# Dilated attention, then a binary 3x3 depthwise convolution: block 0's convolution without TensorE, and the residual laid into PSUM

## The chip, the cores and the metric

The kernel runs on one core of one Trainium2 chip. Its time is the device time in microseconds, the median of several runs; lower is better. The engines are named TensorE (PE in the profile), VectorE (DVE), ScalarE (ACT), GpSimd (POOL) and SyncE (SP, which issues most of the DMAs).

## What is computed

The input is x, 16 images of 56 x 56 pixels with 384 channels, all float32. Two residual layers follow each other:

```python
x = x + conv0(_gn(x), w_qkv, w_proj, b_proj)   # layer 0
x = x + conv1(_gn(x), w)                       # layer 1
# _gn: per image, 32 groups of 12 channels, mean and variance over pixels and channels of the group
# conv0: qkv = einsum('bchw,oc->bohw'); 3 dilations (1, 2, 3) of 128 channels, 4 heads of 32 each;
#        for each pixel softmax over its 9 dilated neighbours of q.k / sqrt(32), then the weighted sum of v;
#        then einsum('bhwc,oc->bhwo', y, w_proj) + b_proj
# conv1: depthwise 3x3, zero padding, the weights replaced by their signs
```

## The kernel before

**Tiling.** Channels lie on the 128 partitions, so an image has three channel blocks (0, 1, 2). Pixels lie along the free axis. A chunk is 8 rows of one image, 448 pixels; an image has 7 chunks, the whole input 112. Each chunk m goes through three plans.

- `plan_a` (lines 494 to 547) loads the chunk, turns it to channels on partitions (`pt_x`, L515), copies it out (L528), takes the statistics of layer 0's normalisation (L530) and stores it as `xd`.
- `plan_b` (549 to 762) is layer 0. It loads and normalises xn (L563), projects k, v (`pkv`) and the queries (`pq`, both L567), copies k and v out (L580) and exchanges their border rows with the neighbouring chunks by DMA (L588, L589). For each of 9 combinations of dilation and neighbour row VectorE multiplies q and k for three neighbours at once (`t`, L632), and TensorE sums over the head's channels (`ps`, L613). The softmax goes through a copy (`sT`, L652), a transpose (`pt_s`, L656) and VectorE and ScalarE steps; the weights, split into three bfloat16 terms (L675 to L683), are transposed by a DMA (`aT`, L686). For each of 9 combinations TensorE spreads the weights over the head's channels (`pb_a`, L700), VectorE multiplies them by v (`w`, L711), and GpSimd adds up (L721, L724, L725 to `y`). `out_project` (731 to 750) multiplies y by the projection weights (`po`, L738); VectorE adds the bias and the residual `xr` (L743) and takes the statistics of layer 1's normalisation (L747); SyncE stores the chunk as `x1d` (L750).
- `plan_c` (775 to 1000) is layer 1, and starts ten chunk steps later, once the image's statistics are there. Block 2's taps are made by ScalarE from a normalised, padded copy (`zg`, L912; `m`, L934) and summed by GpSimd (L944, L949, L952). Blocks 0 and 1 work on `x1`, which isn't normalised: the scale and offset of the normalisation go into per-channel scalars `cs` (`column_scalars`, L764), and ScalarE lays the middle tap, the residual and the offset into a PSUM tile `pc` (`column`, L852). TensorE adds columns of taps to it (`convolve`, L862): it multiplies a packed copy `z`, which holds three shifted rows of 32 channels on 96 partitions (loaded by three DMAs per block, L814, and normalised by ScalarE, L829), by diagonal matrices `kdiag`. Of block 1 it makes the left and the right column of taps (8 products, four at a time on separate quarters of the array), of block 0 the right column only (`LEFT = (0,)`, 4 products). VectorE adds the rest in place (L880) and writes the last tap's result back to x1 (L883): 5 instructions for block 0, 2 for block 1. Then TensorE turns the chunk back (`pt_o`, L961), ScalarE copies it (`osb`, L967), SyncE stores it (L970).

**The last image** (index 15) has its own forms: block 2's nine taps are on VectorE (`taps_last`, L925), and z lies in buffers of other pools (`z_last`).

**PSUM.** Pool `ps_mt` has two banks, which pkv, pt_x, pt_s, po, pt_o and the statistics' products share in turn; `ps_q` has two for pq and pc; `ps_s` has one for ps and the exponentials; `ps_bc` holds one pb_a of three banks. Two products at the start (`open_banks`, L1018) write ps_q's banks over 448 columns.

**Order.** Each piece of work of a chunk has a time in the table `WHEN` (lines 35 to 66), in units of which `STEP` = 9 make a chunk. Chunk m's piece is emitted at its time plus 9 m (plan_c: plus 90 more). The pieces are sorted by time, and between times 81 and 1022 each engine's instructions are pinned in this order (`pin`, L1046), SyncE's queue too. Outside it the framework's scheduler orders by priority. A piece of several stages is a generator: each `yield` ends a stage, and each stage has its own time. The engines run in order and wait on semaphores.

Of the kernel before, what the change touches and what calls it, by code (L numbers as in the profile page):

```python
# [8 lines left out]
F32 = mybir.dt.float32  # L9
# [8 lines left out]
P = 128  # L18
HEADS = 4
HD = 32  # L20
# [3 lines left out]
LEFT = (0,)  # L24
# [11 lines left out]
    load_in=[[21.699]],  # L36
    turn_in=[[22.335, 22.469, 24.701, 28.875], [23.943, 25.409, 27.06, 27.63], [28.352, 28.363, 28.599,
        33.075]],
    load_x=[[-7.77]],
    normalise=[[-1.597], [-3.05], [-3.143]],  # L40
    k=[[1.392, 1.555, 1.762], [3.751, 3.762, 5.408], [3.97, 4.507, 7.411]],
    v=[[11.109, 11.185, 12.149], [14.632, 15.913, 18.706], [17.166, 18.74, 20.057]],
    query=[[10.432], [14.052], [17.994]],
    score=[[11.334], [12.68], [13.826], [14.44], [15.484], [16.643], [18.961], [18.981], [19.283]],
    burst=[[15.151], [18.93], [19.682]],
    softmax=[[20.163, 20.314, 20.448, 20.459, 20.882, 20.893, 21.29, 21.784, 22.998, 23.194]],
    weigh=[[24.063, 24.321, 27.605], [27.904, 27.915, 28.335], [28.245, 28.256, 28.346], [28.64, 28.697,
        28.708], [28.701, 29.148, 29.922], [29.172, 29.776, 32.964], [30.222, 30.929, 35.033], [31.47, 31.924,
        35.101], [33.982, 34.952, 36.663]],
    load_residual=[[37.899]],  # L50
    out_project=[[38.334, 38.803, 38.814, 140.965], [39.193, 39.204, 39.638, 45.624], [39.633, 39.644, 40.418,
        44.585]],
    load_g=[[23.473]],
    normalise_g=[[28.853]],
    taps=[[29.551, 30.093], [30.192, 30.638], [31.25, 32.971]],
    sums=[[36.467], [36.6], [36.611]],
    load_x1=[[21.201]],
    load_z=[[16.673, 19.532], [15.429, 23.495]],
    normalise_z=[[21.293, 22.164], [23.971, 24.249]],
    column=[[21.708], [24.774]],  # L60
    convolve=[[22.545, 23.258], [24.904, 25.733]],
    turn_out=[[36.858, 36.869, 36.88], [37.053, 37.1, 37.526], [37.486, 37.56, 37.792], [37.575, 37.599,
        39.723]],
    statistics=[[47.11, 48.584, 52.665, 52.676, 53.263, 53.274, 54.624, 54.703, 54.714, 54.82, 55.967, 56.105,
        56.694, 57.245, 57.256]],
# [6 lines left out]
def dilated_attention_then_binary_conv(  # L72
# [78 lines left out]
    PARTS = JG * NQ  # L151
# [34 lines left out]
    kcol = const.tile([P, JG, 6], F32, name="kcol")  # L186

    kdiag = const.tile([K3, 2, JG * NQ, HD], F32, name="kdiag")
# [19 lines left out]
    packed = to_pack[:, : JG * P].rearrange("p (j g) -> p j g", j=JG)  # L208
    fold = to_pack[:, JG * P : (JG + 1) * P].rearrange("p (a c) -> p a c", c=HD)
    nc.gpsimd.memset(to_pack, 0.0)  # L210
    for part in range(PARTS):
        j, q = divmod(part, NQ)
        g0, c0 = part * HD // GN_CH, GN_G + 4 * part
        for g in range(NG):
            nc.gpsimd.tensor_copy(gsel[:, g, c0 : c0 + 4], gsel[:, g, g0 : g0 + 4])
        nc.gpsimd.tensor_copy(packed[q * HD : (q + 1) * HD, j, c0 : c0 + 4], gsel[q * HD : (q + 1) * HD, j, g0 : g0 + 4])
# [6 lines left out]
    for j in range(JG):  # L223
        nc.tensor.matmul(
            pz[:, :P], packed[:, j], fold.rearrange("p a c -> p (a c)"), start=(j == 0), stop=(j == JG - 1)
        )
# [79 lines left out]
    def small_weights():  # L306
# [31 lines left out]
        up, mid, down = (ktap[:, :JG, o] for o in (1, 4, 7))  # L338
        nc.vector.tensor_add(kcol[:, :, 0], mid, down)
        nc.vector.tensor_add(kcol[:, :, 1], kcol[:, :, 0], up)  # L340
        nc.vector.tensor_add(kcol[:, :, 2], up, mid)
        by_row = ktap[:, :JG].rearrange("p j (y x) -> p j y x", x=3)[:, :, :, 0]
        for of, ys in ((0, (1, 2)), (1, (0, 1, 2)), (2, (0, 1))):
            for n, y in enumerate(ys):
                nc.vector.tensor_add(kcol[:, :, 3 + of], by_row[:, :, y], kcol[:, :, 3 + of if n else of])
# [7 lines left out]
        for kx in (0, 2):  # L353
            nc.vector.tensor_tensor(
                kdiag[:, kx // 2],
                kp[:, kx, : JG * NQ].unsqueeze(2).to_broadcast([K3, JG * NQ, HD]),
                eye3.unsqueeze(1).to_broadcast([K3, JG * NQ, HD]),
                ALU.mult,
            )
# [20 lines left out]
    def group_norm(sets):  # L380
# [70 lines left out]
        mrz = both[:K3, n_mr:].rearrange("p (j q s) -> p j q s", j=JG, q=NQ) if n_z else None  # L451
# [15 lines left out]
    def put(t0, what, piece):  # L467

        places = WHEN[what]
        for n, stages in enumerate(places):  # L470
            of_it = (n,) if len(places) > 1 else ()
            if len(stages) == 1:
                at(t0 + stages[0], lambda of_it=of_it: piece(*of_it))
                continue
            steps = piece(*of_it)
            for when in stages:
                at(t0 + when, lambda steps=steps: next(steps, None))
# [71 lines left out]
    def plan_b(m, t0):  # L549
# [181 lines left out]
        def out_project(j):  # L731
# [4 lines left out]
            po = ps_mt.tile([P, 512], F32, tag="mt", name="po")  # L736
            for g in range(NG):
                nc.tensor.matmul(  # L738
                    po[:, :PX], wprojT[:, g, j * P : (j + 1) * P], had[f"y{g}"], start=(g == 0), stop=(g == NG - 1)
                )  # L740
            yield
            xr = had["xr"]
            nc.vector.scalar_tensor_tensor(  # L743
                xr[:, j, :], po[:, :PX], bias[:, j : j + 1], xr[:, j, :], op0=ALU.add, op1=ALU.add
            )
# [18 lines left out]
    def column_scalars(b):  # L764

        mr = mr1[b][0]
        cs = st_p.tile([P, JG, 12], F32, tag="cs", name="cs")
        scale, offset = mr[:, :JG, 1:2], mr[:, :JG, 0:1]
        nc.gpsimd.tensor_tensor(cs[:, :, 0:3], ktap[:, :JG, 1:NTAP:3], scale.to_broadcast([P, JG, 3]), ALU.mult)
        nc.gpsimd.tensor_tensor(cs[:, :, 6:9], ktap[:, :JG, 0:NTAP:3], scale.to_broadcast([P, JG, 3]), ALU.mult)  # L770
        nc.gpsimd.tensor_tensor(cs[:, :, 3:6], kcol[:, :, 0:3], offset.to_broadcast([P, JG, 3]), ALU.mult)
        nc.gpsimd.tensor_tensor(cs[:, :, 9:12], kcol[:, :, 3:6], offset.to_broadcast([P, JG, 3]), ALU.mult)
        nc.gpsimd.tensor_scalar(cs[:, :, 1], cs[:, :, 1], 1.0, None, op0=ALU.add)
        cs1[b] = cs

    def plan_c(m, t0):
# [5 lines left out]
        def zero(j):  # L782
            for z, _, _ in had[f"z{j}"]:
# [10 lines left out]
        def set_of(j, q):  # L794
            return next(z[:, q - q0] for z, q0, q1 in had[f"z{j}"] if q0 <= q < q1)

        def load(j):
            by_set = x1d[b].rearrange("(j q c) n -> j c q n", q=NQ, c=HD)[j]
            if b < B - 1:
                z = z_p.tile([P, NQ * PX], F32, tag="z", name="z")[:K3].rearrange("p (q n) -> p q n", q=NQ)  # L800
                had[f"z{j}"] = [(z, 0, NQ)]
            else:

                had[f"z{j}"] = []
                for q0 in range(0, NQ, 2):
                    pool, tag = (t_p, "t") if c % 2 == 0 else (w_p, "w") if (j, q0) != (1, 2) else (xr_p, "xr")
                    z = pool.tile([P, 3, PX], F32, tag=tag, name="z_last")[:K3, :2]
                    had[f"z{j}"].append((z, q0, q0 + 2))
            for ky in range(3):
# [3 lines left out]
                for z, q0, q1 in had[f"z{j}"]:  # L813
# [4 lines left out]
            zero(j)  # L818

        def normalise(j):  # L820
            mrz = mr1[b][1]
            for q in range(NQ):
                z = set_of(j, q)
                if q == NQ - 1 and b == B - 1:
                    nc.vector.tensor_scalar(
                        z, z, mrz[:, j, q, 1:2], mrz[:, j, q, 0:1], op0=ALU.mult, op1=ALU.add
                    )
                    continue
                nc.scalar.activation(z, z, AF.Identity, bias=mrz[:, j, q, 0:1], scale=mrz[:, j, q, 1:2])  # L829
            yield  # L830
            zero(j)
# [10 lines left out]
        def column(j):  # L842
# [4 lines left out]
            parts = [(0, 1, 3), (1, ROWS, 4)] if c == 0 else [(0, ROWS, 4)]  # L847
            if c == NCH - 1:
                parts = [(0, ROWS - 1, 4), (ROWS - 1, ROWS, 5)]
            for r0, r1, of in parts:  # L850
                for x0, x_end, more in ((1, W, 6), (0, 1, 0)) if j in LEFT else ((0, W, 0),):
                    nc.scalar.activation(  # L852
                        pcr[:, r0:r1, x0:x_end], x1[:, j, r0 + 1 : r1 + 1, x0:x_end], AF.Identity,
                        bias=cs[:, j, of + more : of + more + 1], scale=cs[:, j, 1:2],
                    )

        def convolve(j):
            pcr = rows(had["pc", j][:, :PX])

            def tap(kx, q):  # L860
                x0, x1 = max(0, 1 - kx), W - max(0, kx - 1)
                return nc.tensor.matmul(  # L862
                    pcr[q * HD : (q + 1) * HD, :, x0:x1], kdiag[:, kx // 2, j * NQ + q, :],
                    rows(set_of(j, q))[:, :, x0 + kx - 1 : x1 + kx - 1], start=False, stop=(kx == 2),
                    skip_group_check=True,
                )

            in_one_go([
                lambda kx=kx, q=q: tap(kx, q) for kx in ((2,) if j in LEFT else (0, 2)) for q in (3, 0, 1, 2)
            ])  # L870
            yield
            x1 = had["x1"][:, j]
            mid = x1[:, 1 : ROWS + 1]
            cs, above, below = cs1[b], 1 if c == 0 else 0, ROWS - 1 if c == NCH - 1 else ROWS
            taps = [(above, ROWS, 0, 0, 0)]
            if j in LEFT:
                taps += [(above, ROWS, 0, 6, 1), (0, ROWS, 1, 7, 1), (0, below, 2, 8, 1)]
            for r0, r1, ky, at_, left in taps:
# [221 lines left out]
```

## Time and profile before

| | |
|---|---|
| median of 3 runs | 5014.38 us (5013.85 to 5015.21) |
| the profiled execution | 5018.26 us, its span from first to last instruction 5015.4 us |
| granted TensorE clock, mean over the span | 0.977 |
| TensorE busy | 4840.0 us, 97% of the span |
| VectorE busy | 4483.8 us, 89% |
| GpSimd busy | 4239.8 us, 85% |
| ScalarE busy | 2571.0 us, 51% |
| DMA, mean | 167 GB/s |

The profile gives busy time by engine, by stretch of the span and by group of instructions. A group's row has the line, the engine, the operation, written tile <- read tiles with their shapes, the number of instructions, then their busy time, the mean of one in ns, and the idle time of the engine just before them with what ended it. A float32 matmul has two records, a bfloat16 one has one. TensorE's weight loads (PEld) are listed apart and lie beside the products. Because matmuls are pipelined and their ends are modelled, the start of the next burst says more about the price of a burst than its length.

### The profile page before, as it was taken

What the parts mean: (1) busy time and instruction counts of PE and PEld (TensorE: products, weight loads), DVE (VectorE), ACT (ScalarE), POOL (GpSimd) and SP (SyncE); (2) the same over time, 40 slices, a digit from 0 to 9 for tenths busy, and PEclk for the clock granted to TensorE, in tenths of its full rate; (3) what the DMA queues carried; (4) which work ended last, traced back from release to release, by engine and by line L of the source; (5) the groups of instructions that cost most, each with busy time, mean ns of one, the idle gap of its engine ahead of it and who ended that gap; (6) DMA issues with size and microseconds to landing.
All of it is one profiled execution on the core that took longest, in us unless ns stands there. A gap on an engine that the chain in (4) does not pass through costs nothing.

```text
span 5015.4 us, 69405 instructions
## 1 busy us (share of the span) xinstructions
PE 4840.0 (97%) x23469; PEld 2230.2 (44%) x23469; DVE 4483.8 (89%) x4711; ACT 2571.0 (51%) x4645; POOL 4239.8 (85%) x2951
## 2 busy tenths in 40 slices
PE   7999999999999999999999999999999999999954
PEld 4444444444444444444444444444444444444421
DVE  4888999999999999999999999999999999999846
ACT  3222555555555555555555555555555555555455
POOL 2677889888898989988888898989989898998970
PEclk9999999999999999999999999999999999999965
DMA  5434666666666666666666666666666666655554
GB/s 173 119 106 125 177 173 175 175 174 177 179 178 177 173 175 171 178 177 177 174 173 175 176 178 179 180 175 171 175 179 175 177 175 177 161 145 146 133 144 142
DMA packets 813945, 836.23 MB, mean 167 GB/s; under 512 B 362643, under 2 KB 782870, under 8 KB 813590
## 3 DMA queue, kind: packets, MB, share of 16 engines
q1 hardware_dynamic: 805606, 819.81, 61.1%
q10 hardware_dynamic: 7984, 12.00, 0.7%
q8 instruction: 185, 3.03, 0.3%
q14 instruction: 170, 1.39, 0.1%
HBM read 477.43 MB, written 231.21 MB: 141 GB/s over the span
## 4 chain that ended last, share of the span: by engine, by line
PE 83%; POOL 7%; issue 2%; DVE 2%; ACT 1%; DMA 0%; SPq 0%; ACTq 0%; POOLq 0%; DVEq 0%
PE pkv L567 27%; PE po L738 14%; PE pq L567 13%; PE ps L613 11%; PE pb_a L700 5%; PE pc L862 5%; PE pt_o L961 3%; POOL w L721 3%; PE pt_x L515 2%; PE pt_s L656 1%; POOL m L944 1%; DVE w L711 1%; DVE t L632 1%; POOL y L724 1%; POOL y L725 1%
## 5 line engine op out<-in xcount | busy, mean ns | idle before, releaser
L721 POOL TENSOR_TENSOR w<-w 128x1344 f32<-128x1344 f32 x672 | 2053.2, 3055 | 148.2 <-DVE w L711 103.3
L711 DVE TENSOR_TENSOR w<-pb_a,v 128x1344 f32<-128x1344 f32 x1008 | 1562.4, 1550 | 200.0 <-PE pb_a L700 125.4
L567 PE MATMUL pkv<-xn,wqkvT 128*128 128x448 f32 x3924 | 1593.2, 546 | 0.0
L632 DVE TENSOR_TENSOR t<-pq,k 128x1344 f32<-128x1344 f32 x1008 | 1546.4, 1545 | 11.8 <-PE ps L613 7.3
L567 PEld LDWEIGHTS pkv<-xn,wqkvT 128*128 128x128 f32 x3924 | 718.7, 190 | 646.9 <-issue 643.7
L944 POOL TENSOR_TENSOR m<-m 128x1344 f32<-128x1344 f32 x210 | 642.6, 3060 | 273.2 <-ACT m L934 273.0
L738 PE MATMUL po<-y,wprojT 128*128 128x448 f32 x2016 | 823.3, 553 | 12.4 <-ACT osb L967 7.6
L567 PE MATMUL pq<-xn,wqkvT 128*128 128x448 f32 x1962 | 808.2, 547 | 0.1
L580 ACT COPY v<-pkv 128x448 f32<-128x448 f32 x336 | 180.0, 536 | 985.2 <-PE pt_o L961 493.4
L613 PE MATMUL ps<-t,sel 128*32 128x448 f32 x6048 | 662.0, 547 | 3.6 <-DVE t L632 2.9
L829 ACT ACTIVATE z<-z,mr 96x448 f32<-96x448 f32 x840 | 569.7, 750 | 7.3 <-DMA z<-x1d 7.3
L934 ACT ACTIVATE m<-zg,ktap 128x448 f32<-128x448 f32 x945 | 549.7, 657 | 5.4 <-POOL m L944 4.7
L567 PEld LDWEIGHTS pq<-xn,wqkvT 128*128 128x128 f32 x1962 | 360.2, 190 | 395.3 <-issue 285.7
L738 PEld LDWEIGHTS po<-y,wprojT 128*128 128x128 f32 x2016 | 359.5, 191 | 347.3 <-issue 256.5
L967 ACT COPY osb<-pt_o 112x384 f32<-112x384 f32 x420 | 191.4, 481 | 433.7 <-PE pt_o L961 420.4
L724 POOL TENSOR_TENSOR y<-w 128x448 f32<-128x448 f32 x336 | 382.4, 1138 | 29.7 <-PE po L738 4.2
L700 PE MATMUL pb_a<-aT,spread 24*128 24x448 bf16 x3024 | 369.5, 360 | 37.2 <-DVE w L711 27.7
L725 POOL TENSOR_TENSOR y<-y,w 128x448 f32<-128x448 f32 x336 | 381.9, 1137 | 26.0
L880 DVE SCALAR_TENSOR_TENSOR pc<-x,cs,pc 128x440 f32<-128x440 f32 (+3 forms) x560 | 375.8, 673 | 26.8 <-issue 8.6
L700 PEld LDWEIGHTS <-spread 24*128 24x128 bf16 x3024 | 99.6, 91 | 462.0 <-issue 396.8
L613 PEld LDWEIGHTS ps<-t,sel 128*32 128x32 f32 x6048 | 169.6, 109 | 297.8 <-issue 286.2
L580 ACT COPY k<-pkv 128x448 f32<-128x448 f32 x336 | 179.4, 534 | 222.6 <-PE pkv L567 220.3
(154 smaller groups left out, 4671.1 us busy)
## 6 DMA issues: line engine op xcount, KB each, us to landing
z<-x1d SPq DMA_DIRECT2D x570, 224.0 KB, 4.4
xr<-xd SPq DMA_DIRECT2D x112, 672.0 KB, 5.8
x1d<-xr SPq DMA_DIRECT2D x112, 672.0 KB, 5.2
xn<-xd SPq DMA_DIRECT2D x109, 672.0 KB, 5.4
xin<-in_x_dram SPq DMA_DIRECT2D x105, 672.0 KB, 6.2
xd<-xa SPq DMA_DIRECT2D x315, 224.0 KB, 3.4
out_dram<-osb SPq DMA_DIRECT2D x420, 168.0 KB, 3.4
x<-x1d SPq DMA_DIRECT2D x80, 560.0 KB, 4.6
```

Of the source, the lines that this page charges most:

```text
L567: nc.tensor.matmul(dst[:, :PX], wqkvT[:, cc, o0 : o0 + P], had["xn"][:, cc, :], start=(cc == 0), stop=(cc == NG - 1))
L613: return nc.tensor.matmul(had["ps"][32 * j : 32 * j + 32, :PX], sel[:, s0 : s0 + 32], tk, start=(issued[j] == 1), stop=(issued[j] == len(r ...
L632: nc.vector.tensor_tensor(t.rearrange("p k (r w) -> p k r w", w=W), q3, k3, ALU.mult)
L700: return nc.tensor.matmul(pb[:, kx, :PX].rearrange("p (s n) -> p s n", s=NSUB), spread[rows_of, v % 2, :], had["a"][rows_of, :, v // 8, :] ...
L711: nc.vector.tensor_tensor(w.rearrange("p k (r w) -> p k r w", w=W), pb[:, :, :PX].rearrange("p k (r w) -> p k r w", w=W), three(kv[1][g][m ...
L721: nc.gpsimd.tensor_tensor(w0, w0, w, ALU.add)
L724: nc.gpsimd.tensor_tensor(y, w0[:, 0], w0[:, 1], ALU.add)
L725: nc.gpsimd.tensor_tensor(y, y, w0[:, 2], ALU.add)
L738: nc.tensor.matmul(po[:, :PX], wprojT[:, g, j * P : (j + 1) * P], had[f"y{g}"], start=(g == 0), stop=(g == NG - 1))
L829: nc.scalar.activation(z, z, AF.Identity, bias=mrz[:, j, q, 0:1], scale=mrz[:, j, q, 1:2])
L934: nc.scalar.activation(rows(t[:, kx]), zp[:, ky : ky + ROWS, kx : kx + W], AF.Copy, scale=ktap[:, JG, o : o + 1])
L944: nc.gpsimd.tensor_tensor(had["m"], had["m"], t, ALU.add)
```

## The change

- Block 0 (`CB = 1` is the only block with products now) has no z, no load of it, no normalisation of it and no products. ScalarE's `column` lays the interior columns and the two border columns with bias scalars of their own (three pieces instead of two), and VectorE adds seven taps in place and writes the eighth back, each tap a stage of its own. `kcol`, `cs`, `kdiag` and the small packing tensors of the statistics change size accordingly.
- `out_project` takes `po` from `ps_q` instead of `ps_mt`. ScalarE first lays residual plus bias into it; the three products add to that (`start=False`); ScalarE copies the sum to `xr`. VectorE's addition is gone; its statistics stay.
- `WHEN` is another table: block 0's convolution has eight stages, the projection five; k's projection of a chunk is emitted at -8.9 to -6.4 instead of 1.4 to 7.4, the store of a chunk of x1 at 30.6 instead of 44.6, the output's stages at 39.6 to 43.4 instead of 36.9 to 39.7. The statistics of the first two images have times of their own.

Core of the diff, with the taps of block 0:

```diff
-LEFT = (0,)
+CB = 1
...
-            po = ps_mt.tile([P, 512], F32, tag="mt", name="po")
+            po = ps_q.tile([P, 512], F32, tag="q", name="po")[:, :PX]
+            xr = had["xr"]
+            nc.scalar.activation(po, xr[:, j, :], AF.Identity, bias=bias[:, j : j + 1])
+            yield
...
-            yield
-            xr = had["xr"]
-            nc.vector.scalar_tensor_tensor(
-                xr[:, j, :], po[:, :PX], bias[:, j : j + 1], xr[:, j, :], op0=ALU.add, op1=ALU.add
-            )
+            yield
+            nc.scalar.copy(xr[:, j, :], po)
             yield
             nc.vector.bn_stats(stats1[b][:, j, c, :], xr[:, j, :])
...
-                for x0, x_end, more in ((1, W, 6), (0, 1, 0)) if j in LEFT else ((0, W, 0),):
+                for x0, x_end, more in ((1, W - 1, 0), (0, 1, 3), (W - 1, W, 6)) if j < CB else ((0, W, 0),):
...
-            in_one_go([
-                lambda kx=kx, q=q: tap(kx, q) for kx in ((2,) if j in LEFT else (0, 2)) for q in (3, 0, 1, 2)
-            ])
-            yield
...
+            if j >= CB:
+                in_one_go([lambda kx=kx, q=q: product(kx, q) for kx in (0, 2) for q in (3, 0, 1, 2)])
+                yield
+                tap(0, 1)
+                yield
+            else:
+                for ky, kx in ((0, 1), (0, 0), (1, 0), (2, 0), (0, 2), (1, 2), (2, 2)):
+                    tap(ky, kx)
+                    yield
+            tap(2, 1, mid)
...
-    query=[[10.432], [14.052], [17.994]],
+    query=[[1.5], [2.982], [3.688]],
...
-    out_project=[[38.334, 38.803, 38.814, 140.965], [39.193, 39.204, 39.638, 45.624], [39.633, 39.644, 40.418,
-        44.585]],
+    out_project=[[23.391, 25.515, 26.174, 27.604, 79.334], [25.765, 26.049, 26.586, 27.934, 68.996], [26.354,
+        27.424, 27.849, 29.998, 30.603]],
...
-    convolve=[[22.545, 23.258], [24.904, 25.733]],
+    convolve=[[27.149, 29.154, 29.175, 29.74, 29.751, 29.762, 29.773, 29.836], [32.213, 32.574, 32.949]],
```

In it `tap(ky, kx, to)` is one VectorE `scalar_tensor_tensor`: a shifted window of x1 times one column of `cs`, plus the PSUM tile, written back to the PSUM tile or to `to`.

## The prediction

> **What bounds the kernel now.** I read the busy time by stretch first, the groups by shape second, then TensorE's and VectorE's timelines over one chunk. Busy time in five stretches, columns as in the heading:
>
> ```profile
> core 0: us, PE busy (x) PEld busy (x) DVE busy (x) ACT busy (x) POOL busy (x), PEclk, DMA share, GB/s
> 1000.00:2000.00 1000.00, 1000.00 (x4912) 463.76 (x4905) 931.00 (x978) 554.28 (x1003) 898.90 (x599) 1.00 0.66 175
> 2000.00:3000.00 1000.00, 999.83 (x4940) 461.51 (x4937) 931.48 (x960) 541.58 (x979) 900.76 (x588) 1.00 0.66 177
> 3000.00:4000.00 1000.00, 999.94 (x4913) 461.95 (x4915) 933.30 (x967) 551.07 (x993) 897.81 (x582) 1.00 0.66 176
> 4700.00:4850.00 150.00, 100.94 (x468) 40.55 (x466) 102.50 (x103) 68.55 (x121) 137.28 (x79) 0.80 0.55 146
> 4850.00:5016.00 166.00, 82.85 (x376) 39.33 (x376) 97.91 (x159) 90.65 (x169) 26.97 (x35) 0.57 0.49 138
> ```
>
> In the long middle TensorE never stands (999.9 of 1000 at full granted clock); VectorE is busy 93%, GpSimd 90%, ScalarE 55%. After 4700 nobody is full: GpSimd leads until 4850 (137 of 150), then the last image's convolution runs as a chain at a clock of 0.57. So TensorE work taken out of the middle shortens it one for one, until another engine fills up.
>
> One chunk: the middle holds 636 score products t (L632), nine to a chunk, so 70.7 chunks in 3000 us and 42.45 us each. Per chunk TensorE has 42.4, VectorE 39.6 (2.9 idle), GpSimd 38.2, ScalarE 23.3.
>
> **What goes from TensorE.** The timeline shows both convolution bursts, with the burst that follows (start, length, records):
>
> ```profile
> 2001.71 1.66 PE L862 MATMUL pc<-z,kdiag 96*32 96x440 f32 x16
> 2003.31 0.36 PE L700 MATMUL pb_a<-aT,spread 24*128 24x448 bf16 x3
> ...
> 2035.87 0.94 PE L862 MATMUL pc<-z,kdiag 96*32 96x440 f32 x8
> 2036.75 2.52 PE L567 MATMUL pq<-xn,wqkvT 128*128 128x448 f32 x6
> ```
>
> Start to start, block 1's eight products (16 records) take 1.60 us, block 0's four take 0.88. The latter vanish: 1344 to 896 products in all. Of 112 chunks 105 belong to images 0 to 14, whose convolution lies under the attention: 105 x 0.88 = **-92.4 us**. The last image's seven lie in the tail.
>
> **What VectorE gets.**
>
> ```profile
> L743 DVE SCALAR_TENSOR_TENSOR xr<-po,bias,xr 128x448 f32<-128x448 f32 x336 | 227.2, 676 | 59.4 <-PE po L738 59.4
> L880 DVE SCALAR_TENSOR_TENSOR pc<-x,cs,pc 128x440 f32<-128x440 f32 x304 | 206.7, 680 | 9.9
> ...
> 2037.77 2.83 DVE L880 SCALAR_TENSOR_TENSOR pc<-x,cs,pc 128x448 f32<-128x448 f32 x4
> 2040.63 0.68 DVE L883 SCALAR_TENSOR_TENSOR x<-x,cs,pc 128x448 f32<-128x448 f32 x1
> 2041.23 1.55 DVE L632 TENSOR_TENSOR t<-pq,k 128x1344 f32<-128x1344 f32 x1
> ```
>
> Block 0's five taps take 3.46 us (2037.77 to 2041.23): a tap behind the tap it builds on starts 0.715 later, before unrelated work 0.60. After: eight taps, of which four follow directly on their predecessor: 4 x 0.715 + 4 x 0.60 = 5.26, so +1.80. The taps from the right-hand column are not in the trace; they have the 440-element shape of the row above (680 ns), so I take that; the ends are 0 and +0.1 each (L925's 448-element form averages 0.78). Three residual additions leave: two at 0.71 and one at 0.60 in the timeline, -2.02. Net -0.2 a chunk: 39.4 of the new 41.57.
>
> **What ScalarE gets.** Three initialisations of po (SBUF to PSUM, bias by pointer): the nearest rows are 657 ns (L934, one pointer) and 727 (L852, into PSUM, two); I take 0.73. Three copies of po at 0.535 (L580's rows); one or two more one-column pieces at 0.35. Four normalisations leave (L829, 2.72 us by the timeline). Sum +1.4: 24.7 of 41.6. Free while its order causes no wait. Behind a waiting initialisation stand v's copy and sT, which TensorE needs.
>
> **DMA and queues.** z goes from 714 to 357 issues on SP, some 70 of 836 MB. The whole run waits 7.3 us for z, DMA is at 66%: worth 0. SP keeps the order store x1, load residual. The residual must now land before ScalarE's initialisation: the store is 5.2 us, the load 5.8; by the order it is in at about 25 us of the chunk and the bank comes free at 28.9. That cover of 4 us gone, ScalarE's whole queue would stand. GpSimd keeps its work. Smaller packing and statistics: 0.
>
> **The new order, walked through one chunk.** The spreads pb_a (L700) have one buffer, so TensorE and VectorE alternate nine times a chunk. I laid out the new order with start-to-start times (projection 2.36, po 2.35, query 2.26, ps 1.56 or 2.39, 0.30 a spread; 1.47 for t or w). Between spreads TensorE has 2.35, 9.34, 4.27, 5.53, 5.17, 3.99, 3.25, 2.35, 2.36 (with spreads 41.3); between products w VectorE has 2.4, 7.7, 4.9, 0.5, 4.4, 1.8, 1.2, 1.7, 1.1 (38.9). No turn makes TensorE wait: the closest are w5 before the seventh spread (0.33 us to spare), w6 before the eighth (0.4), w0 (0.6). The bank of pc that the second query takes is free 1.3 us early, po's initialisations 2 to 4 us early, GpSimd's y 12 us early. One wait is new: sT's copy (0.73 from the end of the scores) has only a spread and one output transpose (0.72) to hide under before pt_s: about 0.1 a chunk, **+10 us** over 100 chunks (ends 0 and +30). Behind pt_s stand po and all the rest.
>
> **Two rules against it.** The trace lays a ScalarE result under block 0's and block 1's matmuls already (L852, then 1344 products that add to it), each bank having been written over the same 448 columns by a query's matmul before. The Trainium skill (PSUM — Partial Sum Buffer, "The four PSUM rules") says that only 0 is a safe seed, any other should go through TensorE by an identity matmul. By that, three products of 0.79 (a third of 2.36) cost 2.36 a chunk against 0.88 saved: +155 us, slower. The kernel's bank use is the case in which the page lets the sum add, and the row shows it, so I take 0. ScalarE: Activation LUTs ("Rules for kernel authors") wants an addition on VectorE: one row of 0.68 there against 0.73 + 0.535 on ScalarE. Left there, with the new taps, VectorE would have 39.6 + 1.8 = 41.4 of 41.57 and the saving would go into waits; ScalarE has 18 us free, so I side with the row.
>
> **Head and tail.** Head: nine weight transposes now stand behind the first statistics instead of three: about -2 (0 to -3). Tail: the attention of a chunk now runs about 1.8 chunks further ahead of the convolution, so five chunks of image 14, not three, remain after the last po, at 9.6 us of GpSimd each. They stand ahead of the last statistics: from the last y to the last image's scalars I get 57 us against 37.7 (4851.8 to 4889.5). But the last y comes earlier: from the last projection (4760) to it 92 us now, 77 in the new order, and some 6 us of TensorE work has moved behind it. The last image's seven chunks take 126 us now, at 17.5 (4947.2, 4965.1, 4983.0), as ScalarE, TensorE, VectorE in turn; without block 0's z and products, VectorE's 19 taps (12 us) and ScalarE's 7 can overlap, 14 to 15: -20. Sum -22; since the order there is the scheduler's, I take **-10** (ends -30 and +25).
>
> Sum against the profiled run: 5018.3 (span 5015.4) - 92.4 + 10 - 2 - 10 = 4924. The runs' median is 3.9 below the profiled run: **4920**.
>
> **Rivals.**
> - *VectorE at 95% gives half back.* For: 39.4 of 41.57, margins of 0.3 to 0.6; a statistics chunk adds 0.9 on VectorE at two places, an edge chunk three pieces on ScalarE. Against: after the first score products VectorE waits again for TensorE (0.5 to 0.8, three times), so lateness isn't carried on. With 0.4 a chunk waited: 4920 + 42 = 4962. Chance 0.14.
> - *The tail gives back.* Five chunks and the statistics come one after the other with nothing won in the last image: +35 on mine, 4955. Chance 0.07.
> - *Slower: the chain of taps holds a bank.* The second query's product (TensorE) needs the bank that block 0's last tap (VectorE) frees, 1.3 us before. Seven taps lie between there and the preceding spread turn; if spread over single places each costs 1.0 instead of 0.66, the last is 2.4 late, TensorE stands 1.1 in each chunk, more than the 0.88 saved. It decides from 0.97 a tap. With everything that shifts behind it 1.5 a chunk: 4920 + 157 = 5077. Against: 0.60 to 0.715 in this very place. Chance 0.12.
> - *It doesn't do what it says:* the burst of four hides under its neighbours' ends and removing it shortens nothing. Against: 0.88 start to start with neighbours on both sides. About 5015; chance 0.03.
>
> The likeliest, 0.64, is 4895 to 4945. The range 4895 to 4990 leaves out the slower case, the unchanged one and about 0.04 below. A difference under 0.2% (10 us) can't be told from none in this measurement. Faster 0.85, same 0.03, slower 0.12.
>
> **What would show it.** Right: TensorE at 99% or more of 1000 to 4000 with 72.1 chunks there (41.6 each), pc's matmuls at 1680 records, VectorE near 94%, ScalarE near 59%. sT's step: TensorE idle before pt_s of about 0.1. Wrong: TensorE idle over 30 us in 3000, waiting for VectorE's pc (the bank) or w (the turns), or for ScalarE's po. Tail: last po to the last image's first pc over 60 us.

## The result, and the profile after

The changed kernel takes 4941.57 us (median of 4 runs, 4939.87 to 4943.71) beside 5014.8 us before (4 runs, 5013.85 to 5017.07): ratio 0.9854, 95% interval 0.9836 to 0.9871, 73 us less. Its profiled execution is its typical one (4940.53 us, span 4938.8). Faster was forecast, and the time lies in the likeliest case's own range; but 22 us of the forecast gain are missing, and the experiments show that the reason given for the gain holds only in part. Each experiment's ratio below is to runs of the kernel before that were taken beside it (5015 to 5016 us).

Busy time by stretch after, columns as before:

```profile
core 0: us, PE busy (x) PEld busy (x) DVE busy (x) ACT busy (x) POOL busy (x), PEclk, DMA share, GB/s
...
2000.00:3000.00 1000.00, 997.96 (x4812) 463.76 (x4812) 929.19 (x979) 585.50 (x1072) 909.91 (x605) 1.00 0.57 162
...
4700.00:4850.00 150.00, 84.11 (x350) 37.62 (x350) 85.58 (x121) 97.43 (x184) 117.71 (x82) 0.65 0.48 137
4850.00:4939.00 89.00, 40.43 (x180) 17.66 (x180) 73.34 (x126) 41.54 (x81) 0.15 (x1) 0.54 0.45 131
```

The taps of block 0 and 1 are one group now, the right-hand ones among them; a tap takes what it took (mean 670 ns, 676 to 680 in the rows before):

```profile
L874 DVE SCALAR_TENSOR_TENSOR pc<-x,cs,pc 128x440 f32<-128x440 f32 (+3 forms) x896 | 598.7, 670 | 72.8 <-ACT pc L850 31.9
```

In the stretches TensorE is still the full engine of the middle (998 of 1000), VectorE is no fuller than it was (929), ScalarE has 585 for 542. So the chunk became shorter with TensorE still full. How much shorter is read from the time between one chunk's copy sT and the next one's:

| | before | after |
|---|---|---|
| a chunk without statistics | 41.95 us | 41.38 us |
| mean of a chunk, chunks 20 to 104 | 42.38 | 41.89 |
| statistics, per image of 7 chunks, above plain chunks | 3.0 | 3.5 |

A plain chunk gains 0.57, the mean chunk 0.49, where the sum of the prediction had 0.78 (0.88 less a wait of 0.1). TensorE's timeline over one plain chunk after shows why (start, length, records):

```profile
2113.48 0.36 PE L695 MATMUL pb_a<-aT,spread 24*128 24x448 bf16 x3
2113.78 2.52 PE L737 MATMUL po<-y,wprojT 128*128 128x448 f32 x6
2116.23 0.36 PE L695 MATMUL pb_a<-aT,spread 24*128 24x448 bf16 x3
...
2122.02 2.52 PE L562 MATMUL pkv<-xn,wqkvT 128*128 128x448 f32 x6
2124.38 2.42 PE L562 MATMUL pq<-xn,wqkvT 128*128 128x448 f32 x6
2126.64 4.67 PE L562 MATMUL pkv<-xn,wqkvT 128*128 128x448 f32 x12
...
2147.41 1.68 PE L863 MATMUL pc<-z,kdiag 96*32 96x440 f32 x16
2148.92 2.43 PE L608 MATMUL ps<-t,sel 128*32 128x448 f32 x22
```

The same burst of six full-height records (128 rows, 448 columns) takes 2.45 us start to start between two spreads (2113.78 to 2116.23), 2.36 with a spread on one side (2122.02 to 2124.38), 2.26 with none (2124.38 to 2126.64). Record by record it is always the same: 0.376 inside a burst, 0.480 for the first record behind a spread, 0.472 for the last one ahead of a spread. A spread uses 24 rows of the array, the products all 128. In the order before, 8 of a chunk's 12 bursts of six stood away from spreads, after it only 4:

```profile
2107.20 4.73 PE L738 MATMUL po<-y,wprojT 128*128 128x448 f32 x12
2111.86 0.36 PE L700 MATMUL pb_a<-aT,spread 24*128 24x448 bf16 x3
...
2126.07 1.71 PE L613 MATMUL ps<-t,sel 128*32 128x448 f32 x16
2127.60 1.66 PE L862 MATMUL pc<-z,kdiag 96*32 96x440 f32 x16
2129.19 0.36 PE L700 MATMUL pb_a<-aT,spread 24*128 24x448 bf16 x3
```

There two projection outputs made one burst of 12, and next to spreads stood score and convolution bursts, which show no price behind a spread (ps starts 0.29 after the spread's start, as every burst does, and its own records keep their spacing; whether the spread's own 0.29 holds a price, no run shows). Counted over a plain chunk, 6 sides of full-height bursts meet a spread or a convolution burst before, 11 after: five more at 0.10. TensorE's chunk, start to start:

| | before | after | difference |
|---|---|---|---|
| block 0's burst | 0.88 | - | -0.88 |
| block 1's burst | 1.60 | 1.51 | -0.09 |
| projections, queries, po (72 records) | 27.74 | 28.17 | +0.43 |
| scores | 5.56 | 5.65 | +0.09 |
| transposes | 3.53 | 3.40 | -0.13 |
| nine spreads | 2.65 | 2.65 | 0 |
| sum | 41.95 | 41.38 | -0.57 |

Block 1's burst is shorter because a score burst follows it now and no spread: its last record takes 0.355 for 0.465.

Over the whole run:

| stretch | before | after | difference |
|---|---|---|---|
| start to chunk 20's first score product | 876.5 | 871.4 | -5.1 |
| to chunk 104's (84 chunks) | 3559.9 | 3518.9 | -41.0 |
| to the last projection | 323.1 | 307.0 | -16.1 |
| to the last y | 92.3 | 75.6 | -16.7 |
| to the last image's scalars | 37.9 | 68.0 | +30.1 |
| to the end | 125.7 | 97.9 | -27.8 |

### The profile page after: what moved, and what is told of

Same layout as the page of the kernel before. It is cut to its first block, busy times and chain, and to the rows that moved or that the text cites. A ratio compares the mean times of both kernels' runs of the same rounds, so it can differ in the third digit from the quotient of the medians.

```text
span 4938.8 us, 67211 instructions
## 1 busy us (share of the span) xinstructions
PE 4768.9 (97%) x22571; PEld 2204.8 (45%) x22571; DVE 4423.9 (90%) x4738; ACT 2705.6 (55%) x4952; POOL 4226.9 (86%) x2903
## 5 line engine op out<-in xcount | busy, mean ns | idle before, releaser
L627 DVE TENSOR_TENSOR t<-pq,k 128x1344 f32<-128x1344 f32 x1008 | 1513.7, 1547 | 108.9 <-PE pq L562 103.2
L737 PE MATMUL po<-y,wprojT 128*128 128x448 f32 x2016 | 845.8, 556 | 2.4 <-ACT po L733 2.4
L874 DVE SCALAR_TENSOR_TENSOR pc<-x,cs,pc 128x440 f32<-128x440 f32 (+3 forms) x896 | 598.7, 670 | 72.8 <-ACT pc L850 31.9
L937 ACT ACTIVATE m<-zg,ktap 128x448 f32<-128x448 f32 x945 | 563.2, 661 | 9.7 <-POOL w L716 0.4
L523 ACT COPY xa<-pt_x 128x448 f32<-128x448 f32 x315 | 167.5, 532 | 639.1 <-PE pt_x L510 618.2
L608 PEld LDWEIGHTS ps<-t,sel 128*32 128x32 f32 x6048 | 181.3, 109 | 322.9 <-issue 280.5
L850 ACT ACTIVATE pc<-x,cs 128x8 f32<-128x8 f32 (+7 forms) x576 | 288.6, 502 | 61.0 <-DVE t L627 24.4
```

Of the source, the lines that this page charges most:

```text
L608: return nc.tensor.matmul(had["ps"][32 * j : 32 * j + 32, :PX], sel[:, s0 : s0 + 32], tk, start=(issued[j] == 1), stop=(issued[j] == len(r ...
L627: nc.vector.tensor_tensor(t.rearrange("p k (r w) -> p k r w", w=W), q3, k3, ALU.mult)
L737: return nc.tensor.matmul(po, wprojT[:, g, j * P : (j + 1) * P], had[f"y{g}"], start=False, stop=(g == NG - 1), skip_group_check=True,)
L874: nc.vector.scalar_tensor_tensor(acc if to is None else to[:, r0:r1], x1[:, r0 + ky : r1 + ky, x0 + kx - 1 : x_end + kx - 1], cs[:, j, 0, ...
L937: nc.scalar.activation(rows(t[:, kx]), zp[:, ky : ky + ROWS, kx : kx + W], AF.Copy, scale=ktap[:, JG, o : o + 1])
```

## The experiments

A plain-chunk time is the time between two copies sT, as above, taken as the median over the chunks without statistics of that run's profile.

**1. Block 0's products out of the kernel before.**

```diff
-            in_one_go([
-                lambda kx=kx, q=q: tap(kx, q) for kx in ((2,) if j in LEFT else (0, 2)) for q in (3, 0, 1, 2)
-            ])
+            if j not in LEFT:
+                in_one_go([lambda kx=kx, q=q: tap(kx, q) for kx in (0, 2) for q in (3, 0, 1, 2)])
             yield
```

> The kernel before with block 0's four right-hand products left out, all else and the order as before (so the right-hand column is missing from block 0's result). In the traces a chunk without statistics takes 41.95 us before and 41.38 after: 0.57 less, although the burst of four stands for 0.88. Theory A (neighbours): the burst itself is worth 0.88, and the new order gives 0.3 back, because its full-height products stand next to spreads at more places, 0.10 us at each side. Then this chunk takes 41.07 and the run 5014.8 - 105 x 0.88 = 4922, or up to 10 less by the last image's chunks. Theory B (the burst was partly hidden, and its removal is worth only 0.57 in any order): 41.38, 4952.

Measured: 5001.53 us, ratio 0.9974 (0.9964 to 0.9984); a plain chunk 41.90. Both theories miss: the removal is worth 0.05 a chunk, and of the 14.6 us by which the profiled run is shorter 10.9 lie behind the last image's scalars. In the middle neither TensorE (988 of 1000) nor VectorE (933) is full now. One stretch of this run, then TensorE with the wait in brackets and VectorE's score product ahead of it:

```profile
2000.00:3000.00 1000.00, 987.56 (x4743) 457.33 (x4736) 932.87 (x964) 542.72 (x981) 898.66 (x588) 1.00 0.65 177
...
2116.49 1.54 DVE L632 TENSOR_TENSOR t<-pq,k 128x1344 f32<-128x1344 f32 x1
...
2117.22 0.36 PE L700 MATMUL pb_a<-aT,spread 24*128 24x448 bf16 x3
2118.09 2.52 PE L567 MATMUL pq<-xn,wqkvT 128*128 128x448 f32 x6 [0.50 <-DVE t L632]
```

Where the burst had stood, TensorE now waits: from spread to query 0.87 for 0.29. The second query needs the bank that VectorE's third score product frees, and the burst had covered the time until then; another 0.25 is lost at the third query. In the kernel before the bank came free just in time:

```profile
2118.78 1.54 DVE L632 TENSOR_TENSOR t<-pq,k 128x1344 f32<-128x1344 f32 x1
...
2119.80 0.95 PE L862 MATMUL pc<-z,kdiag 96*32 96x440 f32 x8
2120.68 2.52 PE L567 MATMUL pq<-xn,wqkvT 128*128 128x448 f32 x6
```

The score product ends at 2120.32, the query starts at 2120.68: 0.36 us to spare, and at the third query 0.22. TensorE busy 99.99% of the middle did not mean that VectorE's releases left room behind it.

**2. No seed.** The activation that lays residual and bias is deleted, and the products have `start=(g == 0)` for `start=False`, so that residual and bias are missing.

> The kernel after with the projection started on an empty bank: ScalarE doesn't lay residual and bias there, and both are missing from the result. Theory A (the lost 0.3 a chunk is TensorE's neighbours): a plain chunk stays at 41.38, the run within 5 us of 4941.6. Rival C (laying the seed and adding onto it is what costs: ScalarE's 2 us a chunk, the wait for it, or the accumulation): 41.1, about 4910.

Measured: 4947.46 us; a plain chunk 41.39. Laying and adding onto the seed cost nothing in the chunk. (The 6 us lie in the tail: the last image's scalars come at 4846.9 for 4840.9.) Rival C falls.

**3. The residual back on VectorE, in the new order.** The products have `start=(g == 0)` here too.

```diff
-            nc.scalar.activation(po, xr[:, j, :], AF.Identity, bias=bias[:, j : j + 1])
...
-            nc.scalar.copy(xr[:, j, :], po)
+            nc.vector.scalar_tensor_tensor(
+                xr[:, j, :], po, bias[:, j : j + 1], xr[:, j, :], op0=ALU.add, op1=ALU.add
+            )
```

> The kernel after with the residual and the bias added by VectorE again, in the place where ScalarE copies now, and the projection started on an empty bank; the order is otherwise the new one, and nothing is left out. VectorE gets 3 x 0.68 us more in each chunk: 38.8 + 2.0 = 40.8 of 41.38. The prediction held that the saving would then go into waits: a plain chunk at 41.9 or more, the run 4985 to 5040. Rival: VectorE's rests are where they are needed, and it takes the three additions without a wait for TensorE: 41.4, 4945.

Measured: 5007.27 us, ratio 0.9985 (0.9976 to 0.9995); a plain chunk 42.04, as forecast. The third projection output waits for the bank that VectorE's first addition frees:

```profile
2187.82 2.52 PE L736 MATMUL po<-y,wprojT 128*128 128x448 f32 x6 [0.23 <-DVE xr L744]
```

**4. The seed by an identity product.** A product of the identity with xr, `start=True`, ahead of the three; the bias goes into ScalarE's copy.

> The kernel after with the residual brought into PSUM by a product with the identity on TensorE, and the bias added by ScalarE's copy out of PSUM[...]. Nothing is left out. Three products of two records of 0.376 us in each chunk, beside products of the same shape: 3 x 0.752 = 2.26 a chunk, a plain chunk at 43.6, the run 4941.6 + 112 x 2.26 = 5195, slower than the kernel before. Rival: part of it hides under waits of the present order, up to 0.1 a chunk: 5184.

Measured: 5187.17 us, ratio 1.0343 (1.0323 to 1.0364); a plain chunk 43.64, which is 41.38 + 2.26. Work added to TensorE in the new order counts one for one; taking work away was not tried there.

**5. Three taps less on VectorE.** In block 0's loop `tap(ky, kx)` only where `kx != 2`.

> The kernel after with block 0's three right-hand taps left out on VectorE (the right-hand column is missing from block 0's result): VectorE has 1.9 us less in each chunk. Theory A: VectorE isn't what holds TensorE in a plain chunk, which stays at 41.38; only the chunks with statistics (3.5 us an image above plain ones, 2.9 before) can gain, so 0 to 9 us in all, 4933 to 4942. Rival V (VectorE near its limit gives back what TensorE saves): 0.2 to 0.4 a chunk, 4900 to 4920.

Measured: 4932.51 us; a plain chunk 41.39, an image of seven 293.2 for 293.2. VectorE has 43 us less in 1000 (886 for 929) and the middle does not move; what the run gains lies behind chunk 104 (6.6 us in the profiled runs, against 1.2 lost ahead of it). Rival V falls: in the new order VectorE's taps do not hold the middle.

**6. One transpose behind the score burst.** In the table `turn_in` of block 0 from 21.032 to 21.1, nothing else.

> The kernel after, in which only the first input transpose of a chunk changes places with the first score burst that follows it: query, burst, transpose, spread in place of query, transpose, burst, spread. No work is added, and by VectorE's timeline the scores are there 0.5 us earlier than needed. Theory A: from the traces' records, query to burst costs 0.10, burst to transpose 0.10 + 0.05, transpose to spread 0.10; now transpose to burst 0.10 and burst to spread 0.10. So +0.14 to 0.15 a chunk: 41.53, +15 us, 4957. Rival D (only work and waits count, the neighbours don't): 41.38, within 3 us of 4941.6.

Measured: 5006.45 us, ratio 0.9981 (0.9971 to 0.999): nearly the whole gain is gone by one exchange. A plain chunk takes 42.00, +0.62 for the +0.15 expected.

```profile
2203.48 2.52 PE L562 MATMUL pq<-xn,wqkvT 128*128 128x448 f32 x6
2205.93 1.71 PE L608 MATMUL ps<-t,sel 128*32 128x448 f32 x16
2207.57 0.60 PE L510 MATMUL pt_x<-ident,xin 112*128 112x112 f32 x4
...
2211.78 0.60 PE L510 MATMUL pt_x<-ident,xin 112*128 112x112 f32 x4 [0.18 <-ACT osb L970]
```

The sides cost what was expected: query to burst 2.45 for 2.36, transpose to spread 0.54 for 0.48. Of the rest 0.40 is waiting. The transpose comes 1.6 later, so does its copy on ScalarE; four normalisations (2.7 us) stand behind that, the output copy behind those, and the next transpose waits for the bank that the output copy frees. ScalarE in this stretch:

```profile
2208.21 0.53 ACT L523 COPY xa<-pt_x 128x448 f32<-128x448 f32 x1 [4.39 <-PE pt_x L510]
2208.64 2.72 ACT L827 ACTIVATE z<-z,mr 96x448 f32<-96x448 f32 x4
2211.27 0.83 ACT L970 COPY osb<-pt_o 112x384 f32<-112x384 f32 x2
```

**7. The same, with the normalisations behind the output copies.** `normalise_z` from 30.327, 30.374 to 30.67, 30.68.

> The kernel after with the transpose behind the first score burst, as in the experiment that came out at 42.00 a chunk, and ScalarE's four normalisations of z (2.8 us) planned behind the two output copies that they stood ahead of. In that experiment the records showed +0.15 at the transpose's and burst's sides, as forecast, and 0.46 of waits: the transpose's copy on ScalarE came later, the normalisations behind it, the output copy behind them, and a transpose waited for that copy's bank. Theory A (each change of shape on TensorE costs 0.10): without those waits +0.15, a plain chunk at 41.53, 4957. Rival D (no price for neighbours): 41.38, 4942; and if ScalarE's queue isn't what made the waits: 42.0, 5006.

Measured: 4984.86 us, ratio 0.9936 (0.9921 to 0.9951); a plain chunk 41.60.

```profile
2188.95 2.52 PE L562 MATMUL pq<-xn,wqkvT 128*128 128x448 f32 x6
2191.41 1.71 PE L608 MATMUL ps<-t,sel 128*32 128x448 f32 x16
2193.05 0.60 PE L510 MATMUL pt_x<-ident,xin 112*128 112x112 f32 x4
...
2196.91 0.55 PE L510 MATMUL pt_x<-ident,xin 112*128 112x112 f32 x4
```

The wait for the output copy is gone, and with it 0.40. Of the +0.22 left, 0.15 are the changed sides, as theory A has it, and 0.07 lie in the six records of output transposes behind the spread (0.77 for 0.70), which no run explains. That the neighbours have a price of about 0.1 a side, with no work added, is thus shown; ScalarE's queue made the waits. The total missed its 4957 by more: the chunks with statistics lose a further 0.7 an image (4.2 for 3.5), and the remainder lies outside the chunks compared.

**8. Is VectorE's load what held the old order?** Experiment 1, and `nc.scalar.copy` in place of VectorE's additions.

> The kernel before, in its own order, with block 0's four products left out as in the first experiment, and with ScalarE copying the projection out of PSUM in place of VectorE's three additions (so the right-hand column, the residual and the bias are missing). In the first experiment the plain chunk stayed at 41.90: the burst's 0.88 came back as 0.57 of waiting at the same place, ahead of the second query, whose bank is freed by VectorE's third score product, plus 0.25 of waits behind it. Between the third projection output and that score product VectorE has 5.6 us without a rest, one addition of 0.68 among them. Theory E (VectorE's steps are the limit right behind TensorE in the old order, and moving the additions to ScalarE is what lets the saving through): the wait goes, a plain chunk at 41.1 to 41.2, 4920 to 4930. Rival F (the old order's turns between the engines hold it whatever VectorE has to do, only the new order helps): 41.6 to 41.9, 4980 to 5000.

Measured: 5076.21 us, ratio 1.012 (1.0105 to 1.0135); a plain chunk 42.50. It can't answer the question, since a new wait appears:

```profile
2237.50 2.52 PE L567 MATMUL pkv<-xn,wqkvT 128*128 128x448 f32 x6 [0.57 <-ACT xr L743]
```

The projection's bank in `ps_mt` is held by the copy, late in ScalarE's queue (0.83 a chunk), and some 0.5 more is waited ahead of the third query; the wait ahead of the second query is gone. So with this copy, in the old order and pool, the chunk is 0.55 longer than before although the products are gone too.

**9. The same question with nothing in exchange.** Experiment 1, and the additions deleted.

> The kernel before, in its own order, without block 0's four products and without VectorE's three additions; nothing reads the projection out of PSUM (so the attention's result and the right-hand column are missing). The run with a copy on ScalarE in their place came out at 42.50 a chunk, because a projection then waited for that copy's bank (0.84 and 0.48 a chunk): it could not answer the question, though the wait ahead of the second query was gone. Here no engine gets anything in exchange. Theory E (VectorE's steps stand right behind TensorE in the old order; the additions' leaving lets the saving through): no wait ahead of the second query, a plain chunk at 41.05 to 41.1, 4915 to 4925. Rival F (the order's turns hold it whatever VectorE has to do): 41.6 or more, 4975 or more.

Measured: 4988.38 us, ratio 0.9944 (0.9927 to 0.996); a plain chunk 41.67: rival F. The wait ahead of the second query is gone, and one of the same kind stands ahead of the third:

```profile
2208.74 2.52 PE L567 MATMUL pkv<-xn,wqkvT 128*128 128x448 f32 x6
2211.58 2.52 PE L567 MATMUL pq<-xn,wqkvT 128*128 128x448 f32 x6 [0.32 <-DVE t L632]
```

VectorE in the same stretch:

```profile
2200.12 1.56 DVE L711 TENSOR_TENSOR w<-pb_a,v 128x1344 f32<-128x1344 f32 x1 [2.19 <-PE pb_a L700]
2201.60 2.83 DVE L876 SCALAR_TENSOR_TENSOR pc<-x,cs,pc 128x448 f32<-128x448 f32 x4
2204.46 0.68 DVE L879 SCALAR_TENSOR_TENSOR x<-x,cs,pc 128x448 f32<-128x448 f32 x1
```

VectorE had just rested 2.19 us for TensorE; then it has w, block 0's five taps in one piece (3.46 us) and t, w, t, statistics, t before the third query's bank is free. So it isn't short of time over the chunk; by this trace the five taps in one piece are what makes it late here, though no run moved them alone in the old order. The additions' leaving gains 0.23 a chunk over experiment 1, so they count there too. In the kernel after, which gives VectorE more of these taps and not fewer, they lie singly, in pairs and once three in a row between the turns:

```profile
2119.48 1.55 DVE L706 TENSOR_TENSOR w<-pb_a,v 128x1344 f32<-128x1344 f32 x1
...
2122.00 1.38 DVE L874 SCALAR_TENSOR_TENSOR pc<-x,cs,pc 128x440 f32<-128x440 f32 x2
2123.29 1.55 DVE L706 TENSOR_TENSOR w<-pb_a,v 128x1344 f32<-128x1344 f32 x1
2124.76 1.39 DVE L874 SCALAR_TENSOR_TENSOR pc<-x,cs,pc 128x440 f32<-128x440 f32 x2
2126.84 1.56 DVE L627 TENSOR_TENSOR t<-pq,k 128x1344 f32<-128x1344 f32 x1 [0.69 <-PE pq L562]
```

and the score product waits for TensorE, not TensorE for it.

**10 to 12. The tail: the last image's statistics earlier.** The statistics' time less 16 for the last image, and its convolution less 16, 0 or 6:

```diff
-        statistics(STEP * (NCH * b + NCH - 1), [(1, b)] + ...)
+        statistics(STEP * (NCH * b + NCH - 1) - (EARLY if b == B - 1 else 0), [(1, b)] + ...)
...
-            t0 += max(0, WHEN["statistics"][0][-1] + 1.1 - 36)
+            t0 += max(0, WHEN["statistics"][0][-1] + 1.1 - 36 - CONV)
```

> The kernel after with the last image's statistics, and the steps that follow them, planned 16 units earlier, so that they stand ahead of the convolution of image 14's last chunks in TensorE's and GpSimd's queues. In the trace the statistics' inputs are there at 4782, and TensorE takes their first product at 4814, behind transposes that wait for GpSimd. Nothing is left out. Theory T (the queue's order holds the last image, not the work): the last image starts some 25 us earlier, part of it lost to the work that now lies beside it: 4921, between 4910 and 4932. Rival: image 14's leftover work on GpSimd and ScalarE only moves behind, and the end stays: 4941.

> The kernel after with the last image's statistics planned 16 units earlier, its convolution where it was; nothing is left out. With both moved by 16 the scalars came 25 us earlier (4815.7 for 4840.9), but the last image's work then stood ahead of image 14's last chunk on ScalarE, that chunk's last sum came 24 us later and the run was 19 us longer. Theory T: with only the statistics moved the scalars come at about 4816, and the last image starts behind image 14's last sum (4836) and not behind its own scalars: 5 to 10 us less, 4931 to 4937. Rival: nothing is gained, since what follows them stays in its place: 4941.

> The kernel after with the last image's statistics planned 16 units earlier and its convolution 6 units earlier; nothing is left out. Theory T: the scalars at about 4816, and the first chunk of the last image beside image 14's last one: 10 to 18 us less than after, 4923 to 4931. Rival: as with both moved by 16, the two images' work mixes in ScalarE's queue and image 14's last chunk is held: 4941 to 4960.

Measured: 4960.3 us (both by 16; there the last image's padded copy replaces image 14's before that is read, so image 14's block 2 is made of other data, with the same work), 4940.81 (statistics alone), 4953.68 (16 and 6). The reason for trying them, TensorE after, where the statistics' inputs are ready at 4782:

```profile
4814.47 1.44 PE L392 MATMUL pm<-ch,gsel 128*128 128x1 f32 x6
...
4844.56 3.16 PE L863 MATMUL pc<-z_last,kdiag 96*32 96x440 f32 x16 [3.77 <-ACT pc L850]
```

With the statistics alone moved the scalars come at 4813.1 for 4840.9, and the end stays where it was (span 4938.8): ScalarE now waits for them ahead of image 14's work, image 14's last sum comes at 4844.6 for 4836.4, and the last image's first product at 4845.5 for 4844.6. With the convolution moved too, image 14 and the last image mix in ScalarE's queue, and the end comes 13 to 20 us later. Theory T falls: in none of the three orders could the 32 us for which the statistics wait be won. No run with the whole computation beats the changed kernel by more than can be told (4940.81 beside 4941.57).

## Why the prediction was right or wrong

**Right in sign and near in size; the reason given holds only in part.** Against the profiled runs the change gives 76.6 us of span, where the sum had 94.4. Up to the last projection the run won 62.2 where the sum has 84.4 (92.4 and 2, less 10); behind it 14.4 for 10. The rule in the next paragraph would have forecast as much for experiment 1, which gained 13 to 15 us: that the forecast came near here is owed to the new order, which the prediction had walked through turn by turn, and not to the rule.

**"TensorE work taken out of the middle shortens it one for one, until another engine fills up": failed as a reason.** In the order in which that profile was taken the same removal gives 0.05 a chunk (experiment 1), and no other engine fills up: VectorE's score products free two banks of the queries only 0.2 to 0.4 us before TensorE takes them. The margins were computed for the new order, and there they held: TensorE waits for VectorE's w for 4.2 us in 3000, where over 30 was to be the sign of being wrong, and VectorE with three taps less changes nothing (5). So the removal alone does not pay, and the new order needs ScalarE's part (3). The new order with block 0's products left in was not run. With 0.88 more TensorE work at the one for one of experiment 4 a plain chunk would take 42.26 (an estimate), more than the 41.95 before: it is the two together that pay, as far as these runs tell. The rival "it doesn't do what it says" was argued away with 0.88 start to start and neighbours on both sides; in the old order its outcome is nearly what experiment 1 measured, by another cause: the burst hid a wait, not itself.

**-92.4 us: the mis-sized term.** The burst is 0.88, but a plain chunk fell by 0.57. The sum subtracts the burst from the mean chunk's 42.45 (42.38 by the copies sT) as if all else on TensorE kept its length. By the table of TensorE's chunk it did not: +0.43 for projections, queries and outputs, +0.09 for the scores, -0.09 for block 1's burst, -0.13 for the transposes, 0.3 more in all, since what a burst costs depends on what stands beside it. The prediction's layout of the new order, 41.3 plus the wait of 0.1, was close to the plain chunk's 41.38, although it has one duration for each kind of burst (query 2.26 where the three take 2.36, 2.26 and 2.26); but it was used for margins only. Set against the plain chunk before, 41.95, it would have given 0.55. The Trainium skill points the same way (TensorEngine Tiling (Array Packing), "Key Properties" under "Tiling Modes": changing the tiling mode drains TensorE), without a price, and the prediction did not weigh it. The records agree for full-height products beside spreads, 0.10 us a side, and show no price at the start of a score burst behind a spread; that a drain is what the 0.10 us are, no run here shows.

**+10 us for the copy sT: right.** The records show 0.07 a chunk between the output transpose and pt_s (0.18 for 0.11), and pt_s starts 0.05 behind the end of the copy.

**VectorE -0.2: -0.5 measured** (39.5 to 39.0 a chunk, from the busy time of 1000 to 4000). The taps cost +1.80 and the additions' leaving -1.95, as forecast; the other 0.4 are small: w, t and the statistics take 0.01 to 0.04 less each in their new places. **ScalarE +1.4: +1.2** (23.3 to 24.5). **The seed at 0: right** (2). **The identity product's 2.36: 2.26** (4). The sentence that the prediction cites for it (the Trainium skill, PSUM — Partial Sum Buffer, "The four PSUM rules") also allows a second way, to add the seed after evacuation; the kernel before and experiment 3 add behind the product. **The residual left on VectorE: right**, the saving goes into waits (3). **z's transfers at 0** was not tried alone.

**The statistics' chunks: put at nothing in the sum.** They cost 0.5 more an image, some 8 us in all; of it 0.4 is a spread that waits for VectorE's w once an image. It stays with three taps less on VectorE (4.4 us in ten waits, 4.2 in the kernel after), so those taps are not its cause.

**Head -2, tail -10.** Up to chunk 20 the run won 5.1. Layer 1 starts ten chunk steps late, so only nine of block 0's bursts lie there before (9 x 0.49 = 4.4), and the new order puts 26 more records of projections ahead of that point (some 10 us at 0.376 each). These are missing behind chunk 104, which makes up much of the 16.1 won there. So the head's own 2 us can't be told from the table. From the last projection on the run won 14.4, by other parts than were named: to the last y 76 (77 forecast), from there to the scalars 68 (57), the rest 98 (106). "Last po to the last image's first pc over 60 us" was to show the tail wrong; it is 65. The last image's chunks made up for it, at 12.4 us each for the 14 to 15 forecast.

**Rivals.** VectorE giving half back and the chain of taps holding a bank are excluded by experiment 5. That the tail gives back is not what happened.

## What to carry to other kernels

A full engine is the bound of the schedule it was measured in; before taking work off it, look for what would be late next at that very place. A busy record can cover another engine's lateness. Lay out both orders by the same start-to-start rule, neighbours included, and compare totals of the same kind of chunk rather than subtract one burst from a mean. Where queues run in order, moving one short instruction by 1.6 us can cost what a whole change gained (experiment 6: 0.62 us a chunk for 0.57): ask what stands behind its consumer.

## What the hardware showed that was not expected

- A change between full-height products and 24-row spreads costs TensorE 0.10 us on each side (0.480 and 0.472 for 0.376 a record, the same in hundreds of records), a change from score bursts of 32 columns to transposes or spreads as much (0.470 and 0.472 for the last record, 0.356 inside), but a score burst or a convolution burst behind a spread starts without a price that the records show.
- ScalarE's seed in PSUM followed by products that only add costs no time on TensorE beside products that start an empty bank: 41.38 and 41.39 us a chunk.
